# One order of VectorE's blocks in all iterations, two pairs moved between accumulators, and parameters in two transfers

## The chip, the cores and the metric

The kernel runs on one core of one Trainium2 chip. The metric is the device time of one execution in microseconds (us). The kernel before takes 501.95 us (median of three runs, 501.07 to 502.08). A profile shows one execution: five engines (TensorE or PE, with its weight loads listed apart as PEld; VectorE or DVE; ScalarE or ACT; GpSimd or POOL; SyncE or SP, which here only issues transfers) and the DMA engines. Each engine works through its own queue in order and waits for others through semaphores.

## The reference

A stack of four modulated one-dimensional convolutions with a residual, for 128 samples of 64 channels by 1024 positions:

```python
def _layer(x, style, w, b, mw, mb, typ):
    s = style @ mw.T + mb
    weight = SCALE * w * s[:, None, :, None]
    demod = lax.rsqrt(jnp.sum(weight * weight, axis=(2, 3)) + EPS)
    weight = weight * demod[:, :, None, None]
    if typ == 'same':
        out = vmap(_conv_same)(x, weight) + b
    elif typ == 'upsample':
        out = vmap(_conv_up)(x, weight.transpose(0, 2, 1, 3)) + b
        out = _blur(out, 2.0 * blur_k, (1, 1))
    elif typ == 'downsample':
        xb = _blur(x, blur_k, (2, 2))
        out = vmap(_conv_down)(xb, weight) + b
    return out

out = x
for i, typ in enumerate(('same', 'upsample', 'same', 'downsample')):
    out = _layer(out, style, weights[i], biases[i], mod_w[i], mod_b[i], typ)
return x + out
```

All four layers are linear in x, so for one sample they are together one filter, apart from the few positions at both ends, which are computed layer by layer.

## The kernel before

**Tiling.** Two samples of 64 channels lie on the 128 partitions: a pair p, 64 pairs in all. One iteration q of the main loop (`for q in range(NQ)`, L1061, NQ = 32) has four samples, so the pairs p = 2q and p + 1. Its first half belongs to p, its second to p + 1. Every matmul is 64 by 64 and float32; four of them lie in the four quarters of the array at once.

**The filter of four samples** is built by a chain of stages that runs ahead of the loop: `scale3` (ACT, L335, scales the last layer's weights with the table `tA`), `stage1`, `stage2` and `stage3` (PE, with ACT copying each result out of PSUM with a further table), into `Wf`. `combine` (DVE, L452 to L463 with L450) makes from `Wf` the combinations `H`. The tables come from `par_s` (modulation weights, styles, biases) by way of small operations on all engines, in three parts of samples: `PART[0]` before the loop, `PART[1]` in iteration 0, the rest in later iterations, as entries of the list `EXTRA`.

**The convolution of one pair** takes five products with few multiplications each. Their inputs come from `X`, the pair's data, by these blocks, which the text calls by short names:

- G: `pre1`, DVE, L489 and L494, two differences of planes of X, into one of two G buffers
- T1 and T2: also called in `pre1`, POOL, L500 and L501, from G into the pair's T tile (four tiles in turn)
- T3: `pre2a`, DVE, L512, from X; after it the load of two planes of X for pair p + 4 is issued
- T04: `pre2b`, DVE, L522, from G
- products 1 and 2: `convA12` (PE, L552), with T1, T2 and H; product 3: `convA3` (L561), with T3; into `psA`, and ACT copies product 1 to `m1` (L567)
- the sums: `seed1` and `seed2`, together `seed` (DVE, L573): u, v and y from psA and m1, then Y, two instructions that write into an accumulator in PSUM from psA and u. So the sums read PSUM with one operand
- products 0 and 4: `convB` (PE, L614), with T04 and Wf, added on top of Y. `convB(p)` therefore waits for the sums of p, and the sums of p + 1 wait until the outputs of p have been read from the same accumulator
- `output` (L622): Y and y with scale and bias into o, on ACT, in the last iterations also on DVE; `store` (L634) sends it from SP's queue

The accumulator is the tile Y of two PSUM banks. At the end of the loop pairs 60 and 62 use two one-bank tiles of the pool `ps_w`, which the chain of stages used before (`Y2`, L1130 to L1134), and pair 63 uses a two-bank tile of the pool of psA (L1125); both are first cleared by matmuls with zeros (`zeros_to_y`, L164).

**Order.** It is written out by hand: each engine gets its instructions in the order in which the code makes them. Within the loop DVE's blocks come in this order before: from iteration 3 on, first half T3 and T04 of p + 3, G of p + 4, sums of p + 1; second half T3 and T04 of p + 4, G of p + 5, sums of p + 2, H. Iterations 0, 1 and 2 differ. Iteration 0 has: Y of pair 1; the inverse square roots and `tA` of PART[1] (L1105 to L1107); T3 and T04 of 3; G of 4; sums of 2; H of 2; T3 and T04 of 4; u, v and y of 3; G of 5. Iteration 1 begins with Y of 3.

**Before the loop** PE first works on zeros, then on the modulation (`mod_matmul`, L186), again on zeros, and then on the blurred weights (`blur_matmul`, L290, which needs `par_oi`) that ACT copies to E, and on `stage1(0)`. `blur_matmul` writes two banks, one for each half of the rows, with a plan of five steps for each.

## Time and profile before

| what | us |
|---|---|
| median of three runs | 501.95 |
| the profiled execution | 501.05 |
| its span | 499.2 |
| PE busy | 487.2 |
| DVE busy | 444.0 |
| ACT busy | 322.5 |
| POOL busy | 133.7 |

The span is the part of an execution between its first and its last instruction; about 2 us lie around it. Lines of a stage list give, for a stretch of time, the busy us (and number of instructions) of PE, PEld, DVE, ACT and POOL, then the granted clock of TensorE (1.00 is full speed), the share of the DMA engines and GB/s. Lines of a timeline give the start, the length, the engine, the line of the code, the operation, output and input, and, in brackets, how long the engine had been idle and what ended that. One instruction's length reaches some 0.08 us into the next one's, so steps are counted from start to start. A matmul in float32 has two records.

### The profile page before, as it was taken

How to read it: one execution, taken by the hardware profiler on the slowest of the kernel's cores; microseconds unless marked ns; L12 is line 12 of the kernel's file. 1: busy time of each engine (PE TensorE's matmuls, PEld its weight loads, DVE VectorE, ACT ScalarE, POOL GpSimd, SP SyncE). 2: the span in 40 equal slices, each digit the busy share in tenths (PEclk: the TensorE clock that was granted, in tenths of full speed). 3: DMA queues.
4: the chain of work that ended last, by engine and by line, in shares of the span. 5: the costliest groups of instructions: out<-in, count | busy, mean ns of one | idle time of the engine just before them, and what ended most of it. 6: DMA issues, size and time to landing. Idle time of an engine off the chain costs nothing.

```text
span 499.2 us, 28320 instructions
## 1 busy us (share of the span) xinstructions
PE 487.2 (98%) x12616; PEld 474.9 (95%) x12616; DVE 444.0 (89%) x937; ACT 322.5 (65%) x788; POOL 133.7 (27%) x195
## 2 busy tenths in 40 slices
PE   7999999899999999999999999999999999999994
PEld 5899989899999999999999999999999999999994
DVE  4989999999999979987979998879999889888895
ACT  4546757567666667667667667657667666766643
POOL 2234315345222212212222122212212212221210
PEclk8999999999999999999999999999999999999998
DMA  8125535454444445353445444435355435443123
GB/s 260 46 61 170 178 116 169 144 171 140 147 146 149 145 137 164 126 164 122 144 145 161 127 157 153 144 124 163 125 146 165 141 123 189 148 141 130 69 106 127
DMA packets 37449, 70.90 MB, mean 142 GB/s; under 512 B 4176, under 2 KB 28752, under 8 KB 37328
## 3 DMA queue, kind: packets, MB, share of 16 engines
q1 hardware_dynamic: 37248, 68.85, 43.0%
q8 instruction: 99, 1.62, 1.4%
q10 hardware_dynamic: 80, 0.25, 0.1%
q14 instruction: 22, 0.18, 0.1%
HBM read 35.46 MB, written 33.62 MB: 138 GB/s over the span
## 4 chain that ended last, share of the span: by engine, by line
PE 85%; DVE 11%; issue 1%; ACT 1%; DMA 1%; SPq 0%; DVEq 0%
PE psA L540 29%; PE Y L540 19%; PE psR L383 15%; PE psW L420 13%; PE psS L352 6%; PE psE L780 2%; DVE T L522 2%; DVE G L489 2%; DVE Y L573 2%; DMA par_oi<-in_params_oi 1%; DVE G L494 1%; DVE u L573 1%; DVE T L512 1%; DVE v L573 1%; DVE H L458 0%
## 5 line engine op out<-in xcount | busy, mean ns | idle before, releaser
L540 PE MATMUL psA<-T,H 64*64 64x170 f32 x4608 | 207.9, 304 | 0.5 <-ACT R L330 0.3
L540 PEld LDWEIGHTS psA<-T,H 64*64 64x64 f32 x4608 | 190.8, 133 | 1.4 <-issue 0.8
L540 PE MATMUL Y<-T,Wf 64*64 64x170 f32 x3072 | 141.9, 304 | 3.1 <-DVE Y L573 2.8
L500 POOL TENSOR_TENSOR T<-G 128x342 f32<-128x342 f32 x62 | 57.6, 929 | 318.5 <-DVE G L494 189.7
L540 PEld LDWEIGHTS Y<-T,Wf 64*64 64x64 f32 x3072 | 128.8, 133 | 5.7 <-issue 2.3
L630 ACT ACTIVATE o<-Y,oc,dm 128x340 f32<-128x340 f32 (+1 forms) x126 | 79.8, 634 | 60.1 <-PE Y L540 59.4
L420 PE MATMUL psW<-R,par_oi 64*64 64x256 f32 (+3 forms) x1536 | 100.2, 349 | 0.0
L573 DVE SCALAR_TENSOR_TENSOR Y<-psA,u 128x340 f32<-128x340 f32 (+1 forms) x134 | 66.7, 502 | 35.2 <-ACT o L630 32.9
L383 PE MATMUL psR<-S,E 64*64 64x192 f32 (+1 forms) x2304 | 93.9, 299 | 0.4 <-ACT S L330 0.4
L330 ACT ACTIVATE Wf<-psW,t 128x256 f32<-128x256 f32 (+1 forms) x252 | 75.3, 381 | 23.3 <-PE psW L420 23.1
L420 PEld LDWEIGHTS psW<-R,par_oi 64*64 64x64 f32 x1536 | 86.2, 133 | 3.1
L383 PEld LDWEIGHTS psR<-S,E 64*64 64x64 f32 x2304 | 86.9, 133 | 0.6 <-ACT S L330 0.5
L330 ACT ACTIVATE R<-psR,tC 128x448 f32<-128x448 f32 x63 | 36.5, 630 | 56.0 <-PE psR L383 56.0
L630 ACT ACTIVATE o<-y,oc,dm 128x170 f32<-128x170 f32 x125 | 65.8, 526 | 0.4 <-DVE y L573 0.4
L501 POOL TENSOR_TENSOR T<-G 128x342 f32<-128x342 f32 x62 | 58.6, 946 | 0.0
L522 DVE TENSOR_TENSOR T<-G 128x684 f32<-128x684 f32 x64 | 57.0, 890 | 0.0
L489 DVE SCALAR_TENSOR_TENSOR G<-X 128x688 f32<-128x688 f32 x64 | 56.9, 889 | 0.0
L352 PE MATMUL psS<-wd,par_oi 64*64 64x192 f32 x768 | 46.1, 329 | 0.0
L352 PEld LDWEIGHTS psS<-wd,par_oi 64*64 64x64 f32 x768 | 38.4, 136 | 0.5 <-ACT raw L648 0.3
L567 ACT ACTIVATE m<-psA 128x340 f32<-128x340 f32 x64 | 29.2, 456 | 10.1 <-PE psA L540 4.9
L573 DVE SCALAR_TENSOR_TENSOR y<-psA,v 128x340 f32<-128x340 f32 x64 | 32.7, 511 | 2.2
L494 DVE SCALAR_TENSOR_TENSOR G<-X 128x342 f32<-128x342 f32 x64 | 33.2, 519 | 0.0
(132 smaller groups left out, 384.7 us busy)
## 6 DMA issues: line engine op xcount, KB each, us to landing
out<-o SPq DMA_DIRECT2D x126, 255.0 KB, 2.8
X<-in_x SPq DMA_DIRECT2D x60, 344.0 KB, 3.1
X<-in_x SPq DMA_DIRECT2D x60, 172.0 KB, 3.2
X<-in_x SPq DMA_DIRECT2D x4, 516.0 KB, 6.5
Xe<-in_x_ends SPq DMA_DIRECT2D x1, 512.0 KB, 3.6
par_oi<-in_params_oi SPq DMA_DIRECT2D x2, 208.0 KB, 4.8
out<-o SPq DMA_DIRECT2D x2, 170.0 KB, 2.5
par_io<-in_params_io ACTq DMA_DIRECT2D x1, 240.0 KB, 3.8
```

The costliest lines, as they stand in the source:

```text
L330: nc_a.activation(dst, src, AF.Copy, scale=f)
L352: nc.tensor.matmul(ps[r][cols, k * C : (k + K) * C], woi[rows, 2, k, :], src[rows, :], start=(k == 0), stop=(k == K - 1), skip_group_check ...
L383: nc.tensor.matmul(ps[r][cols, lo * C : (lo + m) * C], E[rows, e + 2, :], src[rows, a, :], start=(n == 0), stop=(n == 8), skip_group_check ...
L420: nc.tensor.matmul(ps[r][cols, (lo - t_lo) * C : (hi - t_lo) * C], woi[rows, 0, k, :], rt[c][rows, lo - k : hi - k, :], start=(k == order[0]),
L489: nc_v.scalar_tensor_tensor(g[:, PL:], X[:, : 2 * PL], 0.5, X[:, PL:], op0=ALU.mult, op1=ALU.subtract)
L494: nc_v.scalar_tensor_tensor(plane(g, 2), plane(X, 3), 0.5, plane(X, 2), op0=ALU.mult, op1=ALU.subtract)
L500: eng.tensor_add(t[:, 2, :NJ], plane(g, 2), plane(g, 1))
L501: eng.tensor_sub(t[:, 3, :NJ], plane(g, 2), plane(g, 1))
L522: nc_v.tensor_sub(t[:, 0:2, :NJ], both(a, PL), both(b, 1))
L540: nc.tensor.matmul(ps[s][cols], w, Ts[p][rows, SLOT[m], j : j + NB], start=(g == 0 and m not in (0, 4)), stop=(g == 2), skip_group_check=True,
L573: nc_v.scalar_tensor_tensor(out, x, f, y, op0=ALU.mult, op1=ALU.add)
L630: nc_a.activation(dst, src, AF.Identity, bias=add, scale=d3)
```

## The change

**The loop.** DVE's blocks come in one order in all iterations. First half: G of p + 4, sums of p + 1, T3 and T04 of p + 3. Second half: G of p + 5, sums of p + 2, H, T3 and T04 of p + 4. In iteration 0 the inverse square roots and tA of PART[1] move behind the second half's T3 and T04, G of 6 and then the sums of pair 3 come behind them, and `scale3(4)` moves on ACT from the end of iteration 0 into the first half of iteration 1, between the outputs of pair 2 and the copies of `stage3(3, 1)`. POOL's tables of PART[1] come after T1 and T2 of 5 rather than ahead of those of 4. On SP's queue the two stores of a pair stand together, and the load that T3 releases comes after them.

**The end.** Pairs 61 and 63 use the two one-bank tiles of the chain, 60 and 62 the tile Y; the tile from the pool of psA and its zeros go. Pair 63's outputs are made in two parts, y first, then both parts of Y in one instruction of 340 columns, rather than in three parts.

**The start.** `par_s` has another order of columns (the modulation's bias before the styles) and comes in two transfers: 276 columns first, 116 columns behind the second half of `par_io` and ahead of `par_oi`. The zeros before the modulation are two rounds of 256 columns on both banks (before: one of 256 and one of 512), between it and the variance two of 192 (before: one of 256, and one of 192 after the variance), and one of 192 comes new between `blur_matmul` and `stage1(0)`. The second bank's plan in `blur_matmul` runs backwards.

```diff
-    nc.sync.dma_start(par_s, params_s)
+    nc.sync.dma_start(par_s[:, :first], params_s[:, :first])
     nc.scalar.dma_start(par_io[T], params_io)
     nc.sync.dma_start(par_io[Bo], params_io)
+    nc.sync.dma_start(par_s[:, first:], params_s[:, first:])
...
+        plan[1].reverse()
...
-    zeros_to_y(2, 256)
-    zeros_to_y(2, 512)
+    zeros_to_y(4, 256)
...
-    zeros_to_y(2, 256)
+    zeros_to_y(4, 192)
...
-    zeros_to_y(2, 192)
...
     blur_matmul(psB)
+
+    for rows, ps in zip(HALF, pm[1]):
+        for cols in HALF:
+            nc.tensor.matmul(ps[cols, :192], Z[rows, :C], Z[rows, :192], start=True, stop=True)
...
         output(p, 1, nc_a if q < NQ - 1 else nc_v)
+        if q == 1:
+            scale3(c + 1)
...
-            for i in (2, 0, 1):
+            for i, j in ((2, 3), (0, 2)):
                 for r, eng in enumerate(BOTH):
-                    output(p + 1, r, eng, ((i, i + 1),))
-                    if i != 2:
-                        store(p + 1, r, slice(0, NB) if i == 0 else slice(NB, HO))
+                    output(p + 1, r, eng, ((i, j),))
+                    store(p + 1, r, slice(i * NB, j * NB))
...
         convA12(p + 2)
-        if q:
-            if q < 3:
-
-                (seed2 if q == 1 else seed)(p + 1)
-            if q < NQ - 2:
-                pre2(p + 3)
-            store(p, 0)
-            pre1(p + 4)
-            store(p, 1)
-            if q > 2:
-                seed(p + 1)
-            if q == NQ - 2:
-                pre2(p + 3)
-        else:
-            store(p, 0)
-            store(p, 1)
-            seed2(p + 1)
-            var_inverse(PART[1])
-            var_newton(PART[1])
-            table_A(PART[1], dm[:, 2, PART[1]])
-            for of in (table_C, vector_c0, table_3, vector_Da):
-                of(PART[1])
-            pre2(p + 3)
-            pre1(p + 4)
+
+        if q == 0:
+            seed2(p + 1)
+        pre1(p + 4)
+        store(p, 0)
+        if q:
+            seed(p + 1)
+        store(p, 1)
+        pre2(p + 3)
...
-            Y2[p + 3] = unit(ps_conv, "Y3")
-            zeros_to_y(2, 2 * NB, p + 3)
...
-            Y2[p + 2] = Y2[p + 4] = banks
-            zeros_to_y(2, 2 * NB, p + 2)
-        if q:
-            pre2(p + 4)
+            Y2[p + 3] = Y2[p + 5] = banks
+            zeros_to_y(2, 2 * NB, p + 3)
+        if q < NQ - 2:
+            pre1(p + 5)
             store(p + 1, 0)
-            pre1(p + 5)
+            seed(p + 2)
             store(p + 1, 1)
-        if q < NQ - 2:
-            seed(p + 2)
+        else:
+            store(p + 1, 0)
+            store(p + 1, 1)
         if s < NQ:
             stage1(s)
-        if s + 1 < NQ:
+
+        if q and s + 1 < NQ:
             scale3(s + 1)
         if c < NQ:
-                combine(c)
+            combine(c)
+        pre2(p + 4)
         if q == 0:
-            store(p + 1, 0)
-            store(p + 1, 1)
-            pre2(p + 4)
+            var_inverse(PART[1])
+            var_newton(PART[1])
+            table_A(PART[1], dm[:, 2, PART[1]])
+            for of in (table_C, vector_c0, table_3, vector_Da):
+                of(PART[1])
...
-        if q == 0:
-            seed1(p + 3)
-            pre1(p + 5)
```

More of the change, by code (lines that the diff above doesn't have):

```diff
@@ L106 @@
     par_oi = const.tile([P, NL * K * C + C], F32, name="par_oi")
-    nc.sync.dma_start(par_s, params_s)
+    first = NM + NL + 16
+    nc.sync.dma_start(par_s[:, :first], params_s[:, :first])
     nc.scalar.dma_start(par_io[T], params_io)
     nc.sync.dma_start(par_io[Bo], params_io)
+    nc.sync.dma_start(par_s[:, first:], params_s[:, first:])
     for rows in HALF:
@@ L112 @@
     mwT = par_s[:, :NM].rearrange("s (l c) -> s l c", l=NL)
-    styT = par_s[:, NM : NM + B]
-    mb = par_s[:, NM + B : NM + B + NL]
+    mb = par_s[:, NM : NM + NL]
+    styT = par_s[:, NM + NL : NM + NL + B]
     bb = par_s[:, NM + B + NL :]
@@ L1188 @@
                 mod.reshape(mod.shape[0], -1),
+                twice(mb.T),
                 cond.T,
-                twice(mb.T),
                 twice(bs.T),
```

## The prediction

> **What bounds the kernel now.** I read the page first, then the list of busy times by stage, then PE's timeline where it is idle, and DVE's and POOL's beside it.

> ```profile
> span 499.2 us, 28320 instructions
> PE 487.2 (98%) x12616; PEld 474.9 (95%) x12616; DVE 444.0 (89%) x937; ACT 322.5 (65%) x788; POOL 133.7 (27%) x195
> ```

> PE is idle for 12 us. The stages say where:

> ```profile
> 0.00:20.00 20.00, 17.42 (x300) 13.33 (x304) 12.24 (x39) 9.46 (x25) 6.92 (x26) 0.91 0.60 189
> 60.00:80.00 20.00, 19.26 (x511) 17.99 (x506) 19.69 (x37) 12.90 (x33) 8.63 (x11) 1.00 0.59 175
> 80.00:100.00 20.00, 18.28 (x477) 17.34 (x472) 19.66 (x45) 11.94 (x29) 5.55 (x9) 1.00 0.39 121
> 200.00:300.00 100.00, 100.00 (x2638) 99.34 (x2633) 89.12 (x183) 66.94 (x164) 23.57 (x27) 1.00 0.46 144
> 480.00:499.20 19.20, 12.94 (x335) 11.89 (x326) 13.01 (x32) 6.79 (x14) 0.00 (x0) 0.91 0.32 116
> ```

> From about 122 us to 485 us PE never rests: an iteration takes 14.40 us there, and no order of DVE can shorten it. Only three places can change: the start, the first iterations, where DVE is busy 19.6 us of 20 and is what PE waits for, and the end. In the first iterations PE waits before convB for the sums:

> ```profile
> 56.05 1.14 PE L540 MATMUL Y<-T,Wf 64*64 64x170 f32 x24
> ...
> 89.30 1.10 PE L540 MATMUL Y<-T,Wf 64*64 64x170 f32 x24 [1.72 <-DVE Y L573]
> ```

> Counted from start to start against the undisturbed steps (72 matmuls of convA 2.60 us, stage2 2.50, convB 1.73), PE is late by 0.48 at 61 us (put to "issue", no engine), and by 0.83 at convB(4), 0.25 at convB(6), 1.97 at convB(7), 0.24 at convB(9), 0.35 at convB(11): 3.64 us that DVE causes. convB(2) at 49.45 and convB(3) at 56.05 are on time. DVE itself is held up by POOL:

> ```profile
> 58.90 0.50 DVE L512 TENSOR_TENSOR T<-X 128x342 f32<-128x342 f32 x1
> 59.32 1.58 DVE L522 TENSOR_TENSOR T<-G 128x684 f32<-128x684 f32 x1
> 60.82 1.58 DVE L489 SCALAR_TENSOR_TENSOR G<-X 128x688 f32<-128x688 f32 x1
> 62.33 0.50 DVE L494 SCALAR_TENSOR_TENSOR G<-X 128x342 f32<-128x342 f32 x1
> ```

> ```profile
> 40.46 0.92 POOL L500 TENSOR_TENSOR T<-G 128x342 f32<-128x342 f32 x1 [6.71 <-DVE G L494]
> 41.34 0.91 POOL L501 TENSOR_TENSOR T<-G 128x342 f32<-128x342 f32 x1
> ...
> 59.12 1.05 POOL L500 TENSOR_TENSOR T<-G 128x342 f32<-128x342 f32 x1 [2.08 <-PE psS L352]
> 60.13 1.54 POOL L501 TENSOR_TENSOR T<-G 128x342 f32<-128x342 f32 x1
> ```

> T04 and G last 0.87 alone (rows L522 and L489 of the groups) and 1.58 here: they and POOL's T1 and T2 take turns, one instruction each. Up to 85 us DVE loses 4.1 us so (six instructions by 0.57 to 0.72). The sums never lose any.

> [...] half clock (0.50) from 7.9 to 11.1 us, after a thin stretch. [...]

> **The change part by part**, on the clock of the profiled execution.

> Steady state: nothing. Read round the loop, the order before (T, G, sums, T, G, sums, H) and after (G, sums, T, G, sums, H, T) is the same cycle; only T3 and T04 belong to a pair that is needed half an iteration earlier. T3 of p + 4 would end about 366.5 in the iteration of 361, its convA3 runs at 371.8; T3 of p + 3 about 372, needed at 377: 5 us of slack each. If that cover were gone, each iteration would pay. SP's loads come later by 5 to 8 us and land 3 us after issue, with over 10 us left.

> First iterations. Both kernels have the same stream up to Y of pair 1 (to 41.27). From there after runs, with steps from the timeline: G4 1.21, T3/T04 of 3 1.21, G5 1.21, sums of 2 2.36, H 2.86, T3/T04 of 4 1.21, inverse roots and tA 1.72, G6 1.21, sums of 3 2.36. Nominally G5 ends at 44.90. But POOL still has T1/T2 of 3 (40.46 to 42.25), and its T1/T2 of 4 fall on T3/T04 and G5, the pattern of 59 us: 0.72 and 1.43, so 2.15 to 2.4; I take 2.2. Y of 2 then ends at 49.5 and convB(2) is late by some 0.15. Y of 3 ends at 41.27 + 15.43 + 2.2 + 0.1 = 59.0, and convB(3), due at 56.05, starts at about 59.15: late by 3.1. It is a new wait, and it comes from tA and G6 standing ahead of the sums. scale3(4) on ACT waits for tA until about 55.4 and pushes the copies of stage3(3,1) to 57.4; PE is waiting then anyway. Afterwards, all due times moved by 3.1: Y4 at 64.1 (due 67.5), Y5 73.7 (74.1), Y6 79.7 (82.7), Y7 88.9 (89.3): no new wait, because T3/T04 now stand behind the sums (1.2 less ahead of each) and the three collisions at 55 to 62 and 75 to 78 are gone. Y9 at 103.9 and Y11 at 118.6 add 0.25. Sum 3.35 against 3.64: -0.3. Bounds of the collisions, 0.7 to 3.6 for c (2.2 taken), move this from -1.8 to +1.1.

> Start. The modulation comes earlier, but blur_matmul waits for the second par_oi (issued 2.42, landed 7.44, the queue full all along), so this earns nothing:

> ```profile
> 7.57 2.04 PE L306 MATMUL Y<-w1s,par_oi 64*64 64x64 f32 x32 [0.49 <-DMA par_oi<-in_params_oi]
> 9.33 2.11 PE L352 MATMUL psS<-wd,par_oi 64*64 64x192 f32 x24
> ```

> The new transfer of 464 B rows ahead of par_oi costs between 0 and one issue (0.45); I take 0.15. The new zeros: 768 columns took 2.84 at the first, slow clock, 256 took 0.66 at full clock, so 192 cost 0.65 slow, 0.35 fast. Blur ends 9.76, zeros 10.4; stage1 then runs slow until about 11.15 (0.75 of 1.9) and fast for the rest (0.6): 11.75 against 11.44. +0.3, between -0.3 and +0.8. If the half clock shifts away altogether it is -1.5. The plan run backwards leaves nine 64-column units in each half behind par_oi, as before: 0.

> End. Y of 60 now waits for the outputs of 59 (478.3), 0.6 later, PE only 0.1. H and T3/T04 of 62 (1.21) now lie in the end, so Y62 ends at 489.4; PE would be free at 488.5 as the zeros (0.57) are gone: convB(62) 489.45 against 489.03. Y63 in two tiles needs 1.06 rather than 1.48, and convB(63) starts at 491.84 against 491.50: +0.34. Then the end of the chain before:

> ```profile
> 491.50 2.00 PE Y L540 x48
> ...
> 493.53 0.50 ACT o L630
> ...
> 494.05 0.46 DVE o L632
> ...
> 494.54 0.50 ACT o L630
> ...
> 495.07 0.46 DVE o L632
> ```

> ACT and DVE read the one tile in turn, 2.0 us. With a tile each they run side by side, 0.63: -1.37. The two last stores are then issued one after the other (0.4), and SP has others just before: I count -0.5 in all, between 0 and -1.0.

> Sum: +0.3 - 0.3 - 0.5 = -0.5: 500.55 beside the profiled 501.05. That execution lay 0.9 below the median; taken from the median, 501.45, and I say 501.4.

> **Rivals.** (1) DVE and POOL meet less than I count, for instance once (0.7): convB(3) is late by 1.6, and all following times move with it: -1.5 further, 499.9. For it: the sums shelter POOL from G5 on. Against: T1/T2 of 4 become ready exactly ahead of T3/T04 and G5. (2) The half clock goes: -1.5 at the start instead of +0.3: 499.6. For: [...] zeros now stand in the gap. Against: they run only after 9.6, when it is slow already. (3) Slower: the sums of 3 become the bound. If each of the six instructions of G4, T3/T04 and G5 meets POOL (0.72 each, 4.3 rather than 2.2), convB(3) is late by 5.2, and nothing later gives it back since only 3.64 were lost before: +2.1, 503.5. It decides from a lateness of 4.6 on; 3.6 is where nothing is won. For: POOL's tables of PART[1] took 2.9 at 43 us and could hold G6 up besides. Against: T3, T04 and G ran beside these tables there with 0.1 lost, and POOL has only two instructions for each pair.

> **How the numbers follow.** A measurement of this kernel tells about 0.2%, 1.0 us, from no change. My forecast (a small change, 500.3 to 502.6): 0.50, of it 0.13 below 500.95 and 0.35 within. Rival 1: 0.17, rival 2: 0.10, all faster. Rival 3: 0.23, of it 0.20 beyond 502.95, 0.03 within. Faster 0.40, same 0.38, slower 0.22 (with 0.02 from the forecast's upper edge). The range 499.5 to 503.2 leaves out the far parts of rivals 2 and 3; the likeliest case's own range is 500.3 to 502.6.

> **What would show it.** PE idle 2 to 3 us before convB(3), near 56 us, and no idle at convB(4) and convB(7); T04 and G of 1.58 near 43 to 47 us and none at 59 to 62 or 75 to 78; 14.40 us an iteration between 122 and 474; stage1 ending near 11.75; the last two outputs side by side. The prediction is wrong if convB(3) is on time (rival 1), if the clock stays full before 11 us (rival 2), or if an iteration after 122 us takes more than 14.5.

## The result and the profile after

The changed kernel takes 503.41 us (median of 20 runs, 501.33 to 504.39), the kernel before 501.11 in the runs beside it. The ratio, 1.0039 with a 95% interval of 1.0027 to 1.0052, agrees with that of the means (503.16 and 501.18), not with that of the medians, since the changed kernel's runs fall into two groups (below). It is slower by 2.3 us in the median and by 2.0 in the mean; 501.4 had been forecast, and the range ended at 503.2. The profiled execution took 504.39 us. Its page:

```profile
span 502.6 us, 28358 instructions
PE 488.6 (97%) x12616; PEld 477.9 (95%) x12616; DVE 444.5 (88%) x934; ACT 322.6 (64%) x787; POOL 133.1 (26%) x195
```

The busy time by stage (busy us of PE, PEld, DVE, ACT, POOL, then the granted clock, DMA share, GB/s):

```profile
0.00:20.00 20.00, 17.06 (x270) 13.19 (x274) 10.94 (x37) 8.18 (x22) 7.15 (x26) 1.00 0.58 172
40.00:60.00 20.00, 17.84 (x473) 16.61 (x464) 19.52 (x38) 13.29 (x35) 10.16 (x14) 1.00 0.57 173
60.00:80.00 20.00, 19.50 (x476) 19.43 (x480) 17.79 (x37) 11.10 (x28) 5.84 (x10) 0.91 0.49 148
80.00:100.00 20.00, 20.00 (x552) 19.79 (x545) 18.11 (x41) 13.88 (x35) 5.90 (x9) 1.00 0.44 145
200.00:300.00 100.00, 100.00 (x2640) 99.36 (x2636) 89.80 (x185) 67.99 (x167) 24.25 (x28) 1.00 0.46 146
```

The steady state is as it was, PE 100 of 100. The waits of before between 80 and 100 us are gone. New are 2.2 us without work between 40 and 60, and a mean clock of 0.91 between 60 and 80. PE's timeline shows the place, and the clock by single microseconds shows what followed:

```profile
60.50 1.24 PE L543 MATMUL Y<-T,Wf 64*64 64x170 f32 x24 [2.66 <-DVE Y L576]
...
61.62 2.01 PE L543 MATMUL Y<-T,Wf 64*64 64x170 f32 x22
63.28 1.94 PE L355 MATMUL psS<-wd,par_oi 64*64 64x192 f32 x24
```

```profile
61.00:62.00 1.00, 1.00 (x30) 1.00 (x23) 0.91 (x2) 0.11 (x1) 0.00 (x0) 0.66 0.89 140
62.00:63.00 1.00, 1.00 (x21) 1.00 (x17) 1.00 (x3) 0.06 (x1) 0.00 (x0) 0.50 0.52 129
63.00:64.00 1.00, 1.00 (x20) 1.00 (x17) 0.96 (x3) 0.29 (x1) 0.25 (x1) 0.50 0.53 187
64.00:65.00 1.00, 1.00 (x22) 1.00 (x18) 0.33 (x1) 1.00 (x3) 1.00 (x2) 0.63 0.64 184
```

The idle time before convB(3) was forecast. The half clock behind it, from 61.3 to 64.7, was not: PE does not wait there, it works at half speed, 20 to 22 records in a microsecond rather than the 34 or 35 of s4_t04 below.

The start, in PE's timeline, with POOL's first use of the second half of `par_oi` as a mark of its landing:

```profile
7.45 2.93 PE L309 MATMUL Y<-w1s,par_oi 64*64 64x192 f32 x36 [1.02 <-ACT w1s L290]
10.16 0.86 PE L918 MATMUL psM<-Z 64*64 64x192 f32 x8
10.80 2.14 PE L355 MATMUL psS<-wd,par_oi 64*64 64x192 f32 x24
```

```profile
8.31 0.32 POOL L665 TENSOR_TENSOR wsum<-par_oi 128x64 f32<-128x64 f32 x1 [2.43 <-DMA par_oi<-in_params_oi]
```

Before, that use stands at 7.60, stage1 at 9.33. The end, in PE's timeline:

```profile
483.74 2.84 PE L543 MATMUL psA<-T,H 64*64 64x170 f32 x72
488.37 1.96 PE L543 MATMUL psA<-T,H 64*64 64x170 f32 x48 [1.79 <-DVE Y L576]
490.12 1.94 PE L543 MATMUL Y<-T,Wf 64*64 64x170 f32 x48
...
495.06 2.10 PE L543 MATMUL Y<-T,Wf 64*64 64x170 f32 x48 [0.39 <-DVE Y L576]
```

Another new wait, 1.79 us, stands ahead of convA12(63). It was in no part of the forecast.

For the comparison of all runs, four marks are read from PE's timeline of each profiled execution: A, the first of the undisturbed blocks of 72 matmuls into psA (iteration 0, second half); B, the same block five iterations later; D, the start of convB(63); E, the span's end. The clock column says whether the clock falls during the wait at convB(3) or convB(7).

| kernel | A | B - A | D - B | E - D | clock falls at | median | before beside it | ratio, 95% interval |
|---|---|---|---|---|---|---|---|---|
| before | 44.36 | 77.51 | 369.63 | 7.70 | - | 501.11 | - | 1 |
| changed | 45.81 | 78.47 | 370.78 | 7.54 | convB(3) | 503.41 | 501.11 | 1.0039, 1.0027 to 1.0052 |
| after_again | 45.04 | 78.45 | 370.96 | 7.05 | convB(3) | 503.43 | 500.42 | 1.0055, 1.0036 to 1.0074 |
| s1_start_only | 45.90 | 77.55 | 369.65 | 7.60 | - | 502.40 | 500.12 | 1.0052, 1.0035 to 1.0068 |
| s2_old_start | 44.13 | 78.42 | 370.77 | 7.18 | convB(3) | 501.77 | 500.12 | 1.0019, 1.0001 to 1.0038 |
| s3_fill24 | 45.26 | 78.03 | 370.90 | 7.31 | - | 503.34 | 500.12 | 1.0061, 1.0048 to 1.0074 |
| s4_t04 | 45.01 | 76.81 | 370.18 | 6.90 | - | 502.16 | 500.12 | 1.0030, 1.0017 to 1.0044 |
| s5_fill12 | 44.74 | 76.69 | 370.77 | 8.00 | - | 502.29 | 500.06 | 1.0039, 1.0026 to 1.0052 |
| s6_it0 | 45.13 | 76.41 | 370.93 | 7.13 | - | 501.39 | 500.06 | 1.0022, 1.0013 to 1.0032 |
| s7_split | 46.82 | 77.53 | 369.65 | 7.70 | - | 501.50 | 500.06 | 1.0024, 1.0006 to 1.0043 |
| s8_zeros | 45.05 | 78.67 | 369.63 | 7.85 | convB(7) | 502.33 | 500.06 | 1.0040, 1.0021 to 1.0059 |
| c2_seed3 | 44.52 | 77.67 | 369.99 | 7.32 | - | 500.82 | 500.42 | 1.0013, 1.0000 to 1.0025 |
| c1_again | 44.12 | 76.73 | 369.98 | 7.17 | - | 499.43 | 500.32 | 0.9983, 0.9972 to 0.9994 |

D - B repeats to 0.02 us in the four profiles with before's loop and end. A and E - D scatter by several tenths.

### The profile page after: what moved, and what is told of

It is laid out like the page before. It is cut to its first block, busy times and chain, and to the rows that moved or that the text cites. A ratio compares the mean times of both kernels' runs of the same rounds, so it can differ in the third digit from the quotient of the medians.

```text
span 502.6 us, 28358 instructions
## 1 busy us (share of the span) xinstructions
PE 488.6 (97%) x12616; PEld 477.9 (95%) x12616; DVE 444.5 (88%) x934; ACT 322.6 (64%) x787; POOL 133.1 (26%) x195
## 3 DMA queue, kind: packets, MB, share of 16 engines
q8 instruction: 99, 1.62, 1.5%
## 4 chain that ended last, share of the span: by engine, by line
PE 84%; DVE 5%; ACT 1%; issue 0%; DVEq 0%
PE psA L543 28%; PE Y L543 20%; PE psR L386 14%; PE psW L423 13%; PE psS L355 6%; PE psE L783 2%; DVE Y L576 1%; DVE T L525 1%; ACT o L633 0%; DVE G L492 0%; DVE G L497 0%; DVE o L635 0%; DVE u L576 0%; DVE v L576 0%; DVE T L515 0%
## 5 line engine op out<-in xcount | busy, mean ns | idle before, releaser
L633 ACT ACTIVATE o<-Y,oc,dm 128x340 f32<-128x340 f32 x125 | 79.6, 637 | 60.5 <-PE Y L543 60.3
L492 DVE SCALAR_TENSOR_TENSOR G<-X 128x688 f32<-128x688 f32 x64 | 56.3, 880 | 2.6
L525 DVE TENSOR_TENSOR T<-G 128x684 f32<-128x684 f32 x64 | 56.3, 880 | 0.0
L576 DVE SCALAR_TENSOR_TENSOR y<-psA,v 128x340 f32<-128x340 f32 x64 | 32.7, 512 | 2.2
L576 DVE SCALAR_TENSOR_TENSOR u<-psA,m 128x340 f32<-128x340 f32 x64 | 32.4, 506 | 1.4 <-ACT m L570 1.4
```

Source lines behind the costliest of these rows:

```text
L492: nc_v.scalar_tensor_tensor(g[:, PL:], X[:, : 2 * PL], 0.5, X[:, PL:], op0=ALU.mult, op1=ALU.subtract)
L525: nc_v.tensor_sub(t[:, 0:2, :NJ], both(a, PL), both(b, 1))
L576: nc_v.scalar_tensor_tensor(out, x, f, y, op0=ALU.mult, op1=ALU.add)
L633: nc_a.activation(dst, src, AF.Identity, bias=add, scale=d3)
```

## Experiments on the wait at convB(3)

**Zeros in the wait.** PE gets work while it waits, and the wait stays.

```diff
         side = SLOTS.get(q)
+        if q == 1:
+            psF = unit(ps_w, "psF")
+            for i in range(24):
+                for cols in HALF:
+                    nc.tensor.matmul(psF[i % 2][cols, :170], Z[HALF[i % 2], :C],
+                                     Z[HALF[i % 2], :170], start=True, stop=True)
         convB(p + 1, (lambda: slot(*side)) if side else None)
```

> The changed kernel with 48 matmuls of zeros into a free bank pair on TensorE ahead of convB(3), in the time in which it waits for the sums of pair 3. The wait stays, only the array doesn't stand idle. Theory (the idle time of 2.7 us lets the clock fall to half from about 61 to 65 us): the clock stays full there, psA of the pair behind stage 1 stands at about 63.3 instead of 64.97, and the time is 1.2 to 1.8 us less than the changed kernel, about 501.9. Rival (the wait alone is the loss, the clock is no part of it): psA stays at 64.9 and the time within 0.3 us of 503.4.

The clock stayed full, but the filler was too long. PE's timeline of that run:

```profile
57.48 4.05 PE L1114 MATMUL psF<-Z 64*64 64x170 f32 x94 [0.18 <-ACT Wf L333]
61.23 0.31 PE L543 MATMUL Y<-T,Wf 64*64 64x170 f32 x2
```

convB(3) stands at 61.23; the wait alone would have let it start 14.69 after A as in s4_t04, at 59.95. The filler so cost 1.3 and saved 1.6. The median, 503.34, is where the rival had it, but with a filler that costs as much as it saves the time does not tell the theories apart. So the loop was cut to 12:

> The changed kernel with 24 matmuls of zeros ahead of convB(3), half of those of s3_fill24: by its trace (96 records in 4.05 us) these take about 2.0 us and end near 59.6, before the sums of pair 3 are there, so that convB(3) isn't held back. Theory (the wait of 2.66 us is cheap in itself, 1.6 us more are lost in those runs in which the clock falls during it): every run shows a mean clock of 0.998 or more, psA of iteration 2 stands 32.7 us after psA of iteration 0 (34.3 with the clock drop), and the time is 1.0 to 1.5 us under the changed kernel's, ratio to before about 1.001. Rival (the clock falls anyway, or the wait alone is the loss): mixed clocks of 0.995 and 0.999 as before, ratio 1.004.

```profile
56.94 2.46 PE L1114 MATMUL psF<-Z 64*64 64x170 f32 x48 [0.17 <-ACT Wf L333]
59.33 1.10 PE L543 MATMUL Y<-T,Wf 64*64 64x170 f32 x24
```

Now convB(3) starts when it would have started anyway, its first 24 records take 1.10, and B - A is 76.69 against 78.47: the mechanism is as the theory says. The time is not: 1.0039 rather than 1.001, and four of eleven runs have a mean clock of 0.996 or 0.997. This mean doesn't say where the clock was low; in the profiled run (0.999) it was low only from 499 us on, behind the last matmul, where it costs nothing, and c1_again below has a profiled run of 0.997 with no drop in the loop: its clock falls at 495.2 us, behind the last matmul too. E - D is the longest of all here, 8.00. So this pair of profiles shows the gain in the stage, and the medians alone (2.23 us above before here, 3.01 for after_again) only point the same way, with overlapping intervals.

**The same wait without the drop.** s4_t04, made for the end (below), happens to answer this better. It has the changed kernel's loop, and its PE timeline and clock read:

```profile
59.70 1.10 PE L543 MATMUL Y<-T,Wf 64*64 64x170 f32 x24 [2.65 <-DVE Y L576]
...
60.67 1.09 PE L543 MATMUL Y<-T,Wf 64*64 64x170 f32 x22
61.54 1.19 PE L355 MATMUL psS<-wd,par_oi 64*64 64x192 f32 x24
```

```profile
61.00:62.00 1.00, 1.00 (x34) 1.00 (x29) 1.00 (x2) 0.23 (x2) 0.00 (x0) 1.00 0.67 154
62.00:63.00 1.00, 1.00 (x35) 1.00 (x31) 0.98 (x3) 1.00 (x3) 0.72 (x1) 1.00 0.46 182
```

The wait is the same, 2.65 us, the clock stays full, and B - A is 76.81 instead of 78.42 to 78.47 in the three profiles with the drop. The drop costs 1.64 us, about half of the 3.41 us that it lasts, and the wait doesn't bring it every time.

**Which run is hit.** The traces' clock records tell it. In each of the 13 traces that are read here, the times between two changes of the clock are whole multiples of 3.4133 us (1, 14, 23, 119, 128, 142 or 143 of them). All changes of a run so lie on one grid, and each drop in the loop lasts one step of it; where the grid stands differs from run to run. PE's time, cut along the grid of each run:

| profile | step of the grid | PE idle in it | clock behind it |
|---|---|---|---|
| changed | 57.91 to 61.32 | 2.59 | half |
| after_again | 56.38 to 59.80 | 2.65 | half |
| s2_old_start | 55.35 to 58.77 | 2.60 | half |
| s4_t04 | 55.64 to 59.05 | 2.01 | full |
| s4_t04 | 59.05 to 62.47 | 0.64 | full |
| s8_zeros (below) | 87.48 to 90.89 | 2.01 | half |
| s7_split (below) | 88.34 to 91.75 | 1.97 | full |

The changed kernel's lines, then those of s4_t04:

```profile
57.91:61.32 3.41, 0.82 (x24) 0.85 (x26) 3.34 (x8) 0.92 (x4) 2.28 (x5) 1.00 0.62 210
61.32:64.73 3.41, 3.41 (x56) 3.41 (x52) 2.88 (x6) 1.20 (x4) 0.98 (x2) 0.50 0.66 154
...
55.64:59.05 3.41, 1.40 (x40) 1.08 (x32) 3.30 (x9) 2.23 (x8) 3.10 (x8) 1.00 0.64 224
59.05:62.47 3.42, 2.77 (x76) 2.80 (x80) 3.33 (x6) 0.81 (x3) 0.69 (x2) 1.00 0.77 241
```

In s4_t04 a point of the grid cuts the wait of 2.65 us into 2.01 and 0.64; in the three others nearly all of it falls into one step. The edge lies near 2.0 us of idle time in a step. The steps at the end of the kernel agree: half clock behind 2.28 (s1_start_only and c1_again) and 2.45 (before), full behind 1.87 (s4_t04) and 1.97 (s7_split). At the start idle time alone doesn't decide: there the clock fell behind steps with 0.92 to 1.11 of it (before, s2_old_start, c2_seed3), in which some of the matmuls have only 16 columns.

> The changed kernel once more, on this chip, for the comparison with the repairs. Theory: ratio to before near 1.004 as found; the runs fall in two groups by their mean clock, near 0.999 and near 0.995, 1.5 to 2 us apart, most of them in the lower one, because the clock falls in the 2.66 us wait at convB(3) in some runs and not in others. Rival (the two groups have another cause, such as the start): the profiled run of a group shows the clock full or fallen between 60 and 65 us without regard to its mean clock.

Six runs: one at a mean clock of 0.999 with 501.08 us, five at 0.995 or 0.996 with 503.28 to 503.88. The 20 runs of the first measurement fall apart in the same way: four at 0.999 with 501.33 to 502.00, sixteen at 0.995 or 0.996 with 502.55 to 504.39. The profiled runs of the low group show the drop at convB(3). In four sets of runs with this wait (changed, after_again, s2_old_start, s4_t04), 47 of 70 are at 0.996 or less. The mean alone doesn't prove a drop in the loop: before's profiled run has 0.993 from its start and its end. But in each set these runs are slower than all the others (in s2_old_start 501.65 or more against 500.40 or less, in s4_t04 501.84 against 500.69). The medians of the two groups lie 2.0 to 2.5 us apart, more than the 1.64 of the profiles; what the rest is stays open.

**The order of iteration 0 as before.** The constants' chain (inverse roots, tA and their tables) goes back to the first half of iteration 0, u, v and y of pair 3 to its end; G of 4 and of 5 take their old places with them:

```diff
         store(p, 1)
+        if q == 0:
+            var_inverse(PART[1])
...
         if q < NQ - 2:
             convA12(p + 3)
             convA3(p + 3)
+        if q == 0:
+            seed1(p + 3)
+            pre1(p + 5)
```

> The changed kernel with VectorE's order of the kernel before in iteration 0 and in the sums of pair 3 (the constants' chain early, the first three sums of pair 3 at the end of iteration 0), the new order from iteration 1 on. Theory: convB(3) starts on time and the clock doesn't fall; part of the later waits of before (convB(4), convB(7)) comes back, 1 to 2.5 us in all, so psA of iteration 5 stands 77.0 to 77.9 us after psA of iteration 0 (78.5 in the changed kernel, 77.5 in the one before), ratio to before 1.001 to 1.003. Rival (the later waits came from the order in the later iterations, not from iteration 0): no wait comes back, distance 76.0, ratio below 1.000.

The wait at convB(3) shrinks to 0.52, and one of 0.55 appears at convB(5). B - A is 76.41, nearer to the rival (76.0) than to the theory (77.0 to 77.9): before's later waits came mostly from the order of the later iterations, and the new order does cure them. The ratio, 1.0022, is what start and end still cost.

## Experiments on the start

> The kernel before with the new start alone (parameters in two transfers, the zero matmuls rearranged, the second blur plan reversed). Theory (the start cost more than the forecast's 0.3 because the second half of the parameters lands later and TensorE runs the blur and the first stage at half clock): the first convA12 and every later stage stand about 1.45 us later than before, 502.3 to 502.7 us against 501.1. Rival (the start's delay is taken up by the waits for VectorE in the first iterations): the delay has gone by iteration 5 and the time is within 0.4 us of before.

The three edits of the start on the kernel before: A at 45.90, B - A as before (77.55), so nothing takes the delay up later. The median is 2.3 us above before's, more than the 1.5 of A and the theory's upper end.

> The changed kernel with the start of before. Theory: 1.45 us less than the changed kernel, about 502.0 us, with the wait of 2.7 us at convB(3) and the one at convA12(63) still there. Rival (the start is taken up later on): 503.4 us as with the new start.

Undone in the changed kernel: A at 44.13, the two waits are still there (2.66 and 1.79), ratio 1.0019, with an interval that overlaps the changed kernel's. By A, both directions say that the start is a loss of its own.

> The kernel before with the parameters in two transfers alone; zero matmuls and blur plan stay. Theory (the extra transfer makes par_oi land later, and everything that follows it): the second half of par_oi lands 0.5 to 0.8 us later, the first psA stands at about 45.0 against 44.36, and the time is 0.5 to 1.0 us more, ratio 1.001 to 1.002. Rival (the zero matmuls and their effect on TensorE's speed are the loss): landings as before, ratio 1.000.

The new order of columns goes with it:

```diff
-    nc.sync.dma_start(par_s, params_s)
+    nc.sync.dma_start(par_s[:, :first], params_s[:, :first])
...
+    nc.sync.dma_start(par_s[:, first:], params_s[:, first:])
```

The second half of `par_oi` is used at 8.14 (7.60 before): its issue moved by one issue of 0.57 us on SP's queue. Stage1 stands at 10.05 (9.33), +0.7. A is later still, for a reason that neither theory had, in PE's timeline:

```profile
10.05 2.17 PE L354 MATMUL psS<-wd,par_oi 64*64 64x192 f32 x24
...
12.91 4.58 PE L385 MATMUL psR<-S,E 64*64 64x192 f32 x72
```

stage2 takes 4.58 us here and 2.82 in before: PE was at half speed until 16.66, where this trace's first clock record begins. What lies before a first record reads 1.00 in the clock column. Its 17 runs range from 499.53 to 505.31.

> The kernel before with the rearranged zero matmuls and the reversed second blur plan alone; one transfer of the parameters as before. Theory: the blur ends at the same distance behind par_oi's landing, only the 0.86 us of zeros between the blur and stage 1 come on top, partly beside the copies: first psA at 44.6 to 45.0, ratio 1.000 to 1.001. Rival (the zeros leave TensorE at half speed from the start to the end of the blur and stage 1): first psA at 45.4 or more, ratio 1.002 or more.

The zero matmuls and the reversed plan alone: `par_oi` lands on time (7.55), yet stage1 stands at 10.04: the blur takes 2.69 from 6.71 at half speed (it lasts 2.92, in the changed kernel 2.93; there a record of 192 columns takes 537 ns in the blur and 521 in stage1 on the mean, and 322 in the stage1 of 200 to 300 us), and the new zeros come on top, 0.64 from start to start (0.86 is the length of their record). A at 45.05 is at the theory's end. The ratio, 1.0040, is far beyond it, and PE's timeline shows one reason:

```profile
90.01 1.19 PE L541 MATMUL Y<-T,Wf 64*64 64x170 f32 x24 [2.01 <-DVE Y L574]
...
92.73 1.99 PE L353 MATMUL psS<-wd,par_oi 64*64 64x192 f32 x24
```

The clock falls in before's own wait at convB(7), 2.01 us here, from 90.9 to 94.3, and B - A grows from 77.51 to 78.67. s7_split waited 2.00 at the same place and kept its clock; the two lie on either side of the edge in the table above.

Each half of the start alone so has stage1 0.7 later than in before; the four profiles with the old start have it between 9.21 and 9.84, so 0.2 to 0.8 is what the traces support. The means of A are 44.28 over the four profiles with the old start and 45.27 over the seven with the new: 1.0 for both together, so they do not add up. Part of why can be read: in s3, s4 and s5 the clock rose during stage1, which took 1.37 to 1.62 rather than 2.14. By the clock records it rose for good between 10.52 and 11.21 in the four profiles with the old start, and between 10.89 and 13.53 in the seven with the new one (means 10.94 and 12.15). Since the rises lie on the grid too, one profile of each half is too few to share the loss out.

## Experiments on the end

psA has two buffers. convA12(63) takes the one that held pair 61, so it waits until the sums of 61 have read it. In the changed kernel H and T3/T04 of 62 stand ahead of these sums, in the kernel before only H does: there T3/T04 of 62 were done at 475.1, the sums of 61 end at 483.88, and PE goes through its convA without a gap.

```diff
+        if q == NQ - 2:
+            pre2b(p + 2)
         pre2(p + 3)
...
-        pre2(p + 4)
+        (pre2a if q == NQ - 3 else pre2)(p + 4)
```

> The changed kernel with T04 of pair 62 moved behind the sums of pair 61 (T3 stays). Theory (convA12(63) waits 1.79 us because the psA buffer that it takes is read by the sums of 61, which stand behind H, T3 and T04 of 62): that wait falls to about 0.9 us and the time by 0.6 to 0.9, to about 502.6. Rival (the end is bound elsewhere, by T3 and T04 of 63 or by the sums of 62 and 63 on VectorE, whose work is the same): the wait moves to convB(62), and the time stays within 0.3 us of 503.4.

```profile
485.13 2.00 PE L543 MATMUL psA<-T,H 64*64 64x170 f32 x45 [1.00 <-DVE Y L576]
...
492.00 2.10 PE L543 MATMUL Y<-T,Wf 64*64 64x170 f32 x48 [0.39 <-DVE Y L576]
```

The wait falls from 1.79 to 1.00, about the length of one T04, and D - B from 370.78 to 370.18. D - B of before is 369.63: half of the loss goes with this one block. The expected median, about 502.6, stood for a before of 501.11; here 502.16 stands beside 500.12, a ratio of 1.0030 whose interval overlaps the changed kernel's, so the gain shows in the profile only. The other half was not taken apart (swapping the banks of 60 to 63 back alone was not tried).

## Repairs together

> The changed kernel with three repairs: the start of before, 24 matmuls of zeros in the wait at convB(3), T04 of pair 62 behind the sums of pair 61. Theory (the losses are the start, the clock drop at convB(3) and the wait at convA12(63), and they add): first psA at 44.2, psA of iteration 5 at 121.0 (121.87 before), convB(63) at 491.2 (491.50 before), time 0.5 to 1.2 us under before, ratio 0.998 to 0.999. Rival (the losses aren't additive, a wait comes back elsewhere): ratio 1.000 to 1.002.

The median of eight executions is 499.22 us against 500.42. One of them, the profiled one, took 1819.92 and isn't read; the ratio of the others is 0.9982 with an interval of 0.9958 to 1.0007. The same kernel ran again:

> The same kernel as c1_fill, since its profiled execution was disturbed and the interval of its ratio holds 1. Theory: as there, first psA at 44.2, psA of iteration 5 at 121.0, convB(63) at 491.2; full clock between 56 and 66 us; ratio 0.998, with an interval that leaves 1 out. Rival: ratio 0.9995 to 1.001.

499.43 against 500.32 us, ratio 0.9983, interval 0.9972 to 0.9994: a little faster than before, and so than the changed kernel with its 1.0039. A, B and D stand at 44.12, 120.85 and 490.83, against 44.2, 121.0 and 491.2 expected. PE's timeline:

```profile
56.34 2.46 PE L1111 MATMUL psF<-Z 64*64 64x170 f32 x48 [0.18 <-ACT Wf L330]
58.73 1.10 PE L540 MATMUL Y<-T,Wf 64*64 64x170 f32 x24
```

So the new order is worth 0.8 us in the first iterations (76.73 against 77.51) once the clock is held, and it comes through when start and end are mended.

The other way is to take the wait itself away, with the sums of pair 3 ahead of the constants' chain:

```diff
         if q == 1:
+            seed2(p + 1)
+            constants()
             scale3(c + 1)
```

> As c1_fill without the zeros; in their place the sums of pair 3 stand ahead of the constants' chain and of G of pair 6, so that the wait itself is taken away. Theory: convB(3) starts within 0.7 us of when TensorE is ready, a short wait for the constants appears in its middle, no later wait comes back; psA of iteration 5 stands 76.0 to 76.8 us after psA of iteration 0 (76.8 in s4_t04, where the wait was there at full clock), time 0.8 to 1.5 us under before, ratio 0.997 to 0.9985. Rival (VectorE's backlog only moves: a wait at convB(4) or convB(7) takes the place of the one at convB(3)): distance 77 or more, ratio 0.999 to 1.001.

```profile
59.12 0.23 PE L688 MATMUL psE<-c0f,wsum 64*64 64x16 f32 x2 [1.71 <-POOL t L263]
...
74.61 1.10 PE L540 MATMUL Y<-T,Wf 64*64 64x170 f32 x24 [1.62 <-DVE Y L573]
```

Beside the kernel before this gains nothing: convB(3) starts on time, but in its middle PE waits 1.71 for the constants that are now late, and 1.62 more at convB(5). B - A is 77.67 and the ratio 1.0013, just above what the rival had; the backlog only moved.

## Where the prediction was right and where it failed

**Steady state: right.** From B on, three iterations take 14.57, 14.56 and 14.40 us, before 14.57, 14.57 and 14.39.

**First iterations, the new wait: right in place, cause and size.** convB(3) starts at 60.50, less the 1.45 that the start is late 59.05; 59.15 was forecast (its nine steps add up to 15.35, not 15.43, which changes nothing). The collisions with POOL are those of the forecast, in DVE's timeline (the same three forms, L497, L525 and L492, took 0.51, 0.87 and 0.87 at 41.32, 39.75 and 40.53; POOL's T1 and T2 run from 42.78 to 44.36 and from 44.88 to 47.44):

```profile
43.50 1.23 DVE L497 SCALAR_TENSOR_TENSOR G<-X 128x342 f32<-128x342 f32 x1
44.66 0.50 DVE L515 TENSOR_TENSOR T<-X 128x342 f32<-128x342 f32 x1
45.08 1.58 DVE L525 TENSOR_TENSOR T<-G 128x684 f32<-128x684 f32 x1
46.75 1.41 DVE L492 SCALAR_TENSOR_TENSOR G<-X 128x688 f32<-128x688 f32 x1
```

The waits at convB(4) and convB(7) are gone, 0.45 is left at convB(11). At full clock B - A is 76.7 to 76.8, so -0.7 to -0.8 where -0.3 was forecast. Rivals 1 and 3 (convB(3) late by 1.6 or by 5.2) are refuted by the same number.

**First iterations, the step that failed.** The forecast counted the wait as 3.1 us late, to be set against 3.64 lost before, as if idle time had one price wherever it lies; the clock entered it at the start only. In the traces the clock changes on a grid of 3.41 us that stands elsewhere in each run, and steps with 2.59 to 2.65 us without work (changed, after_again, s2_old_start) and with 2.01 (s8_zeros) had the half clock behind them. With the wait of 2.65 us or so, 47 of 70 runs have the lower mean clock, 0.996 or less. Several short waits were exchanged for one long one, and the long one costs 1.64 more when the clock goes: +0.95 in place of -0.3, 1.25 of the miss.

**Start: right in mechanism for the transfer, mis-sized, and wrong on the clock.** "Between 0 and one issue (0.45); I take 0.15": it was one whole issue, 0.57 on SP, and 0.7 in the landing of the changed kernel's profile (means of the landing 8.09 over eight profiles with two transfers, 7.65 over five without). The zeros took 0.64 from start to start, as costed. The blur's last 32 records took 1.76 in before and 1.94 to 1.98 in the five profiles where they stand apart. The step that failed is "fast for the rest": stage1 was to run slow only to 11.15, 1.35 us in all, but the clock rose at 13.53, and stage1 took 1.93 from start to start. +0.3 was forecast, +1.0 is the mean of A. Rival 2 (the half clock goes) is refuted: 1.00 in the clock column of the changed kernel's first 20 us hides an array at half speed: stage1's 24 records take 2.14 there, and 1.19 at 61.54 in s4_t04.

**End: a wait overlooked, and stores underrated.** convB(63) was to come 0.34 later; D - B says 1.15. The forecast followed Y, H and T04 but not the second reader of psA: with T3/T04 of 62 put ahead of the sums of 61, convA12(63) waits for its buffer. With half of that order undone it is 0.55. The last outputs do run side by side: the last one ends 2.77 behind convB(63)'s start (before 4.03), -1.26 where -1.37 was forecast. But from there to the end of the span it takes 4.5 on the mean of nine profiles instead of 3.7 on four. The two last stores of 170 KB are now issued together, and the DMA view of the end has 3.0 us to their landing (2.5 before). So -0.5 became about +0.8, 1.3 of the miss.

The sum: +1.0 at the start, +0.95 in the first iterations with the drop (-0.7 without), +0.8 at the end. This is 2.7 with the drop and 1.1 without; at the rate of 47 drops in 70 runs it is 2.2 on the mean, beside a measured 2.0 in the mean and 2.3 in the median. Taken apart, the changed kernel's sixteen runs with the lower clock have a median of 503.59, 2.5 above before, and its four others 501.58, 0.5 above: the sum is 0.2 too high for the one group and 0.6 for the other.

## What to carry to other kernels

Price a wait of TensorE by its length in one piece, not only by the sum: a wait in the loop that put 1.97 us of idle time into one step of 3.41 (s7_split) left the clock full, and the one of 2.65 at convB(3) cost 1.64 us on top where 2.59 or more of it fell into one step. Where such a wait can't be avoided, matmuls of zeros into a free bank that end just before it does are nearly free (in s5_fill12 and c1_again convB(3) starts 14.59 and 14.61 behind A, in s4_t04 without them 14.69); too many delay what follows (1.3 in s3_fill24). When a block is moved, follow every buffer that it reads to its next writer, also at the end of the loop, where the order of the steady state meets different neighbours.
